# Moving one product of each attention block from VectorE to GpSimd, in place

## The chip, the cores and the metric

The kernel runs on one core of a Trainium2 chip. The metric is the device time of one execution in microseconds (us); lower is better. The engines are named as the profile names them: PE is the matrix engine TensorE (PEld its weight loads), DVE is VectorE, ACT is ScalarE, POOL is GpSimd, and SP only issues DMAs.

## The reference

Four graph layers follow one another on x of 16 graphs x 1024 nodes x 128 features, with one adjacency matrix of 1024 x 1024 for all of them (about eight edges a row). Layers L0, L2 and L3 are attention layers, L1 is a graph attention with one head. An attention layer, cut to what matters here:

```
Q, K, V = h @ Wq, h @ Wk, h @ Wv              # 8 heads of 16
scores  = einsum('bnhd,bmhd->bhnm', Q, K) / sqrt(16)
attn    = softmax(where(adj == 0, -inf, scores))
x       = layer_norm(h + einsum('bhnm,bmhd->bnhd', attn, V) @ Wo + bo)
out     = layer_norm(x + relu(x @ W1 + b1) @ W2 + b2)
```

The kernel computes it from the edges alone: for each node it fetches the keys and values of its neighbours, multiplies keys by the query, sums over the 16 features of a head, takes the exponential, and weights the values by it.

## The kernel before

**Tiles.** The nodes are sorted by degree and cut into 8 blocks of 128 (`T`); the graphs are cut into 2 groups of 8 (`GR`), so a row of one group is 8 x 128 = 1024 numbers (`ROW`). A *unit* is one layer, group and block: 64 units, of which 48 are attention. Keys and values of all nodes lie in a table in HBM, 2048 numbers a row. One *chunk* is an indirect DMA that fetches 128 rows of the table, 1 MB, one row for each partition; a partition is one edge. A block is 32 nodes x 4 edges in each of 4 quarters, and each quarter has its own number of full chunks. What is left over of the four quarters is packed into one chunk that they share (`MIX`).

**Parts.** In an attention unit the chunks are worked on in five parts: three pairs of chunks, then the shared chunk alone, then one more pair (`PIECES`, into which the shared chunk is inserted at place 3). So part 3 is half as large as the others: 1024 numbers a partition against 2048.

**The loop** runs over all parts of all units in an order written out by hand. Each part goes through:

- `gathered` (L965, GpSimd): the indirect DMAs of the part three ahead (`i - 1 + AHEAD`, `AHEAD` = 4), into one of four buffers `e`. They are issued after the weighting of part i - 1, which frees the buffer.
- `products` (L977, DVE): keys times queries, from `e` and `qr` into a buffer `pr`, of which there are four. `qr` holds the queries expanded to the edges of each quarter. For the shared chunk the second operand is `qx` instead.
- `exponentials` (L1000 on DVE, then L1004 on ACT): the sum over a head's 16 features into `sc`, then its exponential `ex`.
- `weighted` (L1028, DVE), one iteration later: values times `ex`, from `e` into the same `pr`, over the product.
- `summed` (L1044, PE), two iterations after the product: matmuls that add the edges of a node up in `acc`. Two parts of one rank are summed together, after the second.

DVE's order in a block is thus P0 R0 (W of the part before) P1 R1 W0, then the closing of the unit before it (L1081 and twice L1084), P2 R2 W1 P3 R3 W2 P4 R4 W3, with P for L977, R for L1000, W for L1028.

**`qx`** is one buffer in a pool of one (`queries_of_shared`). `shared(u)` fills it from `qr` with two to four DMAs on SP's queue (L943), in the second iteration of a block, when `qx` is free. SP works in order, and ahead of these copies stand, in layers L0 and L2, the stores of the unit that is being finished (L575, L592, L617), which wait for ACT. In layer L3 there are no such stores, and the results leave by scatters on GpSimd's queue (L699).

**Around it.** While these parts run, PE and ACT also do the rest of the unit before (its projections, norms and feed-forward part) and prepare the queries of the next one, a few steps between the parts. GpSimd also adds each unit's sums into `seen` (L1097), two operands in SBUF of 128 numbers a partition.

Of the kernel before, what the change touches and what calls it, by code (L numbers as in the profile page):

```python
# [18 lines left out]
ALU = mybir.AluOpType  # L19
# [29 lines left out]
ROW = G * D  # L49
# [17 lines left out]
MIX = J  # L67
# [51 lines left out]
def of_piece(v, piece):  # L119

    a, b = piece[0][0], piece[-1][0]
    if len(piece) == 2 and a == b:
        return v[:, a : a + 1].to_broadcast([v.shape[0], 2, v.shape[2]])
    return v[:, a : b + 1 : max(b - a, 1)]
# [21 lines left out]
def sparse_path(ctx: ExitStack, tc: tile.TileContext, a: dict, out: bass.AP, flag):  # L146


    nc = tc.nc
# [64 lines left out]
    def gather_buffer():  # L214
        return gathers.tile([P, max(4 * ROW, J * (ROW + G))], F32, tag="e", name="e")
# [646 lines left out]
    parts = []  # L862
# [7 lines left out]
    es, prs, exs, qs, qx, ofs, accums = {}, {}, {}, {}, {}, {}, {}  # L870

    def is_attention(u):
        return LAYERS[units[u][0]][1] is ATTN
# [76 lines left out]
    def gathered(i):  # L950
        if i >= len(parts):
            return
        u, pieces = parts[i]
        if u == T:
            while slow:
                while busy[0] and not held[0]:
                    advance(tails)
                advance(slow)
        l, g, t = units[u]
        width = tables[l, g].shape[1]  # L960
        many = 2 if is_attention(u) else J
        e = gather_buffer()
        es[i] = e[:, : many * width].rearrange("p (k c) -> p k c", k=many)
        for k, (j, r) in enumerate(sum(pieces, [])):
            nc.gpsimd.indirect_dma_start(  # L965
                out=es[i][:, k, :], out_offset=None, in_=tables[l, g][:, :],
                in_offset=bass.IndirectOffsetOnAxis(
                    ap=idx[:, min(l, 1), t, COLUMN[t, j, r] : COLUMN[t, j, r] + 1], axis=0
                ),
                bounds_check=N - 1, oob_is_err=False,  # L970
            )

    def products(i):
        u, (piece,) = parts[i]
        n = len(piece)
        prs[i] = [prods.tile([P, 2, ROW], F32, tag="pr", name="pr")]
        nc.vector.tensor_tensor(  # L977
            prs[i][0][:, :n, :], es[i][:, :n, :ROW],
            qx[u].rearrange("p (o c) -> p o c", o=1) if (MIX, 0) in piece
            else of_piece(qs[u], piece),  # L980
            ALU.mult,
        )

    def exs_of(i):

        u, pieces = parts[i]
        t = units[u][2]
        c, n = PLACE[(t, *pieces[0][0])], sum(map(len, pieces))
        return exs[u][:, c : c + n, :], n
# [116 lines left out]
    def advance(gens):  # L1106
        for gen in list(gens):
            got = next(gen, "end")
            if got == "end":
                gens.remove(gen)  # L1110
            elif got == "free":
                free.append(gen)
# [58 lines left out]
    with tc.manual_schedule():  # L1171
        wide = [gather_buffer() for _ in range(EDGES)]
        setup, entry, weights = graph(wide), at_once(0), load_weights("L0")
        next(setup)
        next(weights)
        next(entry)
        more = [weights, load_graph_weights()]
        rest = slots()
        first, second = loaded(0), loaded(1)
        for i, room in enumerate(setup):  # L1180
            if i == T:
                for gen in more:
                    next(gen)
            if room == "load":
                next(first)
            elif room == "spread":
                for _ in entry:
                    pass
                next(rest)
            elif room == "slots":  # L1190
                next(rest)
                for _ in first:
                    pass
                for _ in queries(0):
                    pass
                slow.append(at_leisure(1))
            elif room == "gather":
                for k in range(AHEAD - 1):
                    gathered(k)
                next(second)  # L1200
            else:
                for _ in range(room):
                    if next(entry, "end") == "end":
                        advance(slow)
                        break
        scratch.close()
        prods = ctx.enter_context(tc.tile_pool(name="prods", bufs=4))
        smalls = ctx.enter_context(tc.tile_pool(name="smalls", bufs=3))
        nc.gpsimd.memset(wide[3], 0.0)
        gathered(AHEAD - 1)  # L1210
        fronts.extend([islice(rest, WAIT + 2), second] + more)
        closing, sizes = None, ()
        begun = 0
        for i in range(len(parts) + 2):
            here = i < len(parts)
            u = parts[i][0] if here else len(units)
            if here:
                l = units[u][0]
                eager[0] = 1 if u < 2 else 0
                if i and parts[i - 1][0] != u:  # L1220
                    begun = i
                    if u < T - 1:
                        fronts.append(islice(rest, WAIT + 2))
                    if l + 1 < len(LAYERS) and LAYERS[l + 1][1] is ATTN:
                        if units[u][1:] == (0, 1):
                            more = load_weights(LAYERS[l + 1][0])
                            next(more)
                            next(more)
                        if units[u][1:] == (0, 4):
                            fronts.append(more)  # L1230
                if is_attention(u):
                    products(i)
            if i > 1:
                summed(i - 2)
                done = parts[i - 2][0]
                if parts[i - 1 : i] == [] or parts[i - 1][0] != done:
                    closing = divided(done)
                    next(closing)
            others()
            if here:  # L1240
                exponentials(i)
            if here and i == begun + 1:
                if is_attention(u):
                    shared(u)
                while loads:
                    advance(loads)
                if u + 1 < len(units):
                    fronts.append(queries(u + 1))
                loads.append(loaded(u + 2))
                if u:  # L1250
                    advance(loads)
            others()
            if 0 < i <= len(parts):
                weighted(i - 1, 0)
                if not is_attention(parts[i - 1][0]):
                    others()
                    weighted(i - 1, 2)
                gathered(i - 1 + AHEAD)
                for _ in sizes:
                    pass  # L1260
            if closing is not None and here:
                while any(gen not in free for gen in tails):
                    if opening[0] is None:
                        advance(tails)
                    else:
                        planned("ab")
                while opening[0] is not None and opening[0] < len(plan[0]):
                    planned()
                next(closing)
                sizes, closing = closing, None  # L1270
                passes = 3 if is_attention(u) else 4
                steps = STEPS if is_attention(done) else GRAPH_STEPS
                steps -= LATE[units[done][0]]
                pace[:] = 0.0, steps / (passes * sum(part[0] == u for part in parts) - 1)
                if is_attention(done) and opening[0] is None:
                    for gen in list(tails):
                        if gen in free:
                            for _ in gen:
                                pass
                            tails.remove(gen)  # L1280
                opening[0] = 0 if is_attention(done) else None
                plan[0] = PLANS.get(units[done][0], ())
            others()
            if i + 1 >= len(parts) or parts[i + 1][0] != u:

                while fronts:
                    advance(fronts)
        while opening[0] < len(plan[0]):
            planned()
        while tails:  # L1290
            advance(tails)
        for _ in closing:
            pass
        while tails:
            advance(tails)
# [435 lines left out]
```

## Time and profile before

| | |
|---|---|
| median of 3 runs | 2157.91 us (2153.96 to 2158.05) |
| profiled execution | 2143.22 us |
| its span, and mean granted PE clock | 2141.5 us, 0.97 |
| busy: PE, DVE, ACT, POOL | 91%, 86%, 71%, 49% |
| indirect gathers L965 | 576, 1569 ns mean, 8.1 us from issue to landing |
| copies into `qx`, L943 | 114 DMAs; 6.7 us to landing at 256 KB |
| all DMA | 636.10 MB, 297 GB/s over the span |

A row of a group in the profile gives line, engine, operation, output and inputs by their tile names, the shapes as partitions x elements, the count, and then busy us in total and mean ns of one; after the second bar stands the time that the engine was idle just before, and what ended most of it. A row of a timeline gives the start from the span's begin, the duration, engine, line, operation, and in brackets the idle time before it and its releaser. The first 110 us sort the graph, then come L0, L1, L2 and L3; the third layer fills most of 1000 to 1554 us. The durations shown come from this one execution.

### The profile page before, as it was taken

Reading aid. Unit: us, or ns where it says so; the run is one execution under the profiler, and the core shown is the slowest. Engines: PE = TensorE matmul, PEld = TensorE weight load, DVE = VectorE, ACT = ScalarE, POOL = GpSimd, SP = SyncE. Lnnn points to the kernel's source line nnn. Section 1 sums busy time; section 2 is a strip of 40 time slices with the busy share of each in tenths; the row PEclk is TensorE's granted clock in tenths of the full one; section 3 lists DMA queues with packets and bytes.
Section 4 is the critical chain, followed back from the end, with each engine's and each line's share of the span. In section 5 each row is a group of like instructions: output and inputs, shape, how many; then the busy total and the mean of one; then the engine's idle time right before and its main releaser. Section 6 shows DMA issues by size and latency. Waiting matters only on the chain.

```text
span 2141.5 us, 37070 instructions
## 1 busy us (share of the span) xinstructions
PE 1954.5 (91%) x13444; PEld 1237.4 (58%) x13444; DVE 1852.2 (86%) x1368; ACT 1522.8 (71%) x5043; POOL 1048.6 (49%) x699
## 2 busy tenths in 40 slices
PE   6769999999999988997999999999998999898986
PEld 5545666666655555554566565666655555555554
DVE  6977999999997666677899999999998998989993
ACT  3437878878886554555687887778886878776874
POOL 3333445555456576784354544444443545545540
PEclk8789999999999999999999999999999999999998
DMA  7978888988988799998898998989988878687860
GB/s 272 348 271 291 309 300 313 312 287 316 318 314 288 271 324 323 347 376 309 295 338 310 334 312 293 321 324 319 320 303 297 288 277 297 233 311 260 313 227 22
DMA packets 164800, 636.10 MB, mean 297 GB/s; under 512 B 34664, under 2 KB 37480, under 8 KB 116110
## 3 DMA queue, kind: packets, MB, share of 16 engines
q0 software_dynamic: 88720, 485.08, 63.5%
q1 hardware_dynamic: 75888, 148.57, 20.5%
q8 instruction: 108, 1.77, 0.3%
q14 instruction: 84, 0.69, 0.1%
HBM read 581.08 MB, written 92.34 MB: 314 GB/s over the span
## 4 chain that ended last, share of the span: by engine, by line
PE 68%; DVE 11%; ACT 8%; issue 6%; DMA 4%; POOL 2%; POOLq 0%; DVEq 0%; ACTq 0%
PE acc L1044 17%; PE yps L752 7%; PE ps L654 7%; PE ps L738 7%; PE ps L583 6%; PE ps L929 6%; PE yps L728 4%; PE yps L727 4%; DMA e<-table,idx 4%; PE yps L756 3%; DVE pr L1028 3%; PE ps L920 2%; DVE pr L977 2%; DVE sc L1000 2%; ACT qr L932 2%
## 5 line engine op out<-in xcount | busy, mean ns | idle before, releaser
L965 POOL DMA_INDIRECT e<-table,idx x576 | 903.6, 1569 | 899.0 <-DVE pr L1028 708.8
L1028 DVE TENSOR_TENSOR pr<-e,ex 128x2048 f32<-128x2048 f32 (+1 forms) x320 | 662.2, 2077 | 56.8 <-ACT ex L1016 29.6
L1044 PE MATMUL acc<-pr,marks 128*32 128x512 f32 x2656 | 516.1, 605 | 36.3 <-DVE pr L1028 18.3
L977 DVE TENSOR_TENSOR pr<-e,qr 128x2048 f32<-128x2048 f32 x192 | 441.8, 2301 | 83.2 <-PE acc L1044 30.4
L1000 DVE TENSOR_REDUCE sc<-pr 128x128 f32<-128x2048 f32 (+1 forms) x240 | 497.4, 2073 | 8.1
L631 ACT ACTIVATE z<-yps,root 128x128 f32<-128x128 f32 x888 | 312.9, 368 | 70.4 <-PE yps L756 55.6
L1044 PEld LDWEIGHTS acc<-pr,marks 128*32 128x32 f32 x2656 | 109.7, 110 | 297.6 <-issue 246.9
L752 PE MATMUL yps<-W,f 128*128 128x128 f32 x1520 | 253.6, 285 | 16.9 <-ACT f L747 16.9
L752 PEld LDWEIGHTS yps<-W,f 128*128 128x128 f32 x1520 | 203.4, 191 | 99.3 <-ACT f L747 60.2
L647 ACT ACTIVATE z<-yps,rstd 128x128 f32<-128x128 f32 x888 | 251.0, 367 | 1.6
L587 ACT COPY kv<-ps 128x512 f32<-128x512 f32 x176 | 102.8, 588 | 175.3 <-PE ps L583 160.0
L932 ACT COPY qr<-ps 128x512 f32<-128x512 f32 x384 | 202.9, 602 | 22.2 <-PE ps L929 19.9
L583 PE MATMUL ps<-Wkv,xT 128*128 128x256 f32 x768 | 204.1, 409 | 12.7 <-ACT xT L660 5.5
L747 ACT ACTIVATE f<-ps,b 128x512 f32<-128x512 f32 x190 | 130.4, 687 | 87.9 <-PE ps L738 87.8
L738 PE MATMUL ps<-x,W 128*128 128x512 f32 x384 | 187.0, 610 | 1.3 <-ACT x L662 1.3
L631 ACT ACTIVATION_READ_ACCUMULATOR z<-yps,root 128x1 f32 x888 | 184.4, 208 | 0.0
L583 PEld LDWEIGHTS ps<-Wkv,xT 128*128 128x128 f32 x768 | 145.1, 201 | 67.5 <-issue 14.0
L654 PE MATMUL ps<-ident,z 128*128 128x128 f32 x896 | 148.9, 283 | 37.1 <-ACT qr L932 27.5
L654 PEld LDWEIGHTS ps<-ident,z 128*128 128x128 f32 x896 | 106.1, 142 | 89.0 <-ACT qr L932 62.3
L929 PE MATMUL ps<-q,rep 32*128 32x512 f32 x768 | 146.7, 663 | 8.6 <-ACT q L924 7.6
L727 PE MATMUL yps<-Wo,oT 128*128 128x128 f32 x768 | 153.2, 282 | 0.2
L728 PE MATMUL yps<-centre,x 128*128 128x128 f32 x768 | 152.6, 281 | 0.5 <-ACT x L723 0.2
(174 smaller groups left out, 2526.1 us busy)
## 6 DMA issues: line engine op xcount, KB each, us to landing
table<-kv SPq DMA_DIRECT2D x88, 512.0 KB, 7.5
kept<-xT SPq DMA_DIRECT2D x96, 256.0 KB, 5.1
x<-kept SPq DMA_DIRECT2D x48, 512.0 KB, 7.9
qx<-qr SPq DMA_DIRECT2D x54, 256.0 KB, 6.7
e<-table,idx POOLq DMA_INDIRECT x576, 8.1
table<-kv SPq DMA_DIRECT2D x32, 256.0 KB, 8.1
qx<-qr SPq DMA_DIRECT2D x48, 128.0 KB, 5.0
qx<-qr SPq DMA_DIRECT2D x12, 384.0 KB, 4.6
```

The costliest lines, as they stand in the source:

```text
L583: nc.tensor.matmul(ps[:, k, :], x[:, i + k, :], w[LAYERS[l][0], "Wkv"], start=True, stop=True,)
L631: nc.scalar.activation(z[:, i, :], y[:, i, :], AF.Square, scale=D**-0.5, bias=root, accum_out=total[:, i : i + 1],)
L647: nc.scalar.activation(z[:, i, :], y[:, i, :], AF.Copy, scale=rstd[:, i : i + 1])
L654: nc.tensor.transpose(ps[:, i, :], z[:, i, :], ident)
L738: nc.tensor.matmul(ps, p["W1"][:, f * P : (f + 1) * P], x1.rearrange("p g n -> p (g n)"), start=True, stop=True,)
L752: nc.tensor.matmul(ps[:, i, :], f1[:, f, i * P : (i + 1) * P], p["W2"][:, f, :], start=(f == 0), stop=False,)
L929: nc.tensor.matmul(ps, rep_of(j), q[32 * j : 32 * j + 32], start=True, stop=True)
L965: nc.gpsimd.indirect_dma_start(out=es[i][:, k, :], out_offset=None, in_=tables[l, g][:, :], in_offset=bass.IndirectOffsetOnAxis(ap=idx[:, ...
L977: nc.vector.tensor_tensor(prs[i][0][:, :n, :], es[i][:, :n, :ROW], qx[u].rearrange("p (o c) -> p o c", o=1) if (MIX, 0) in piece else of_p ...
L1000: nc.vector.tensor_reduce(sc[:, :n, :], prs[i][0][:, :n, :].rearrange("p k (a d) -> p k a d", d=HD), mybir.AxisListType.X, ALU.add,)
L1028: nc.vector.tensor_tensor(prs[i][k0 // 2][:, :m, :].rearrange("p k (a d) -> p k a d", d=d), es[i][:, k0 : k0 + m, base : base + ROW].rearr ...
L1044: nc.tensor.matmul(outs[32 * j : 32 * j + 32], marks[:, mark, :], rhss, start=(chunk == mine[0]), stop=(chunk == mine[-1]),)
```

## The change

For a shared chunk, `products` no longer does anything: a new function `product_of_shared` multiplies on GpSimd, in place in `qx`, and enters `qx` as that part's product buffer. It is called at the end of each iteration, for the part two ahead, right after the gathers that the iteration issues. The shared chunk is part 3, so the call falls into the iteration of part 1, the same in which `shared(u)` issues the copies into `qx`. From there on the reduction reads `qx`, the weighting writes into `qx`, and the matmuls of `summed` read it; `pr` is used by the four pairs alone.

```diff
     def products(i):
         u, (piece,) = parts[i]
+        if i in prs:
+            return
         n = len(piece)
         prs[i] = [prods.tile([P, 2, ROW], F32, tag="pr", name="pr")]
         nc.vector.tensor_tensor(
             prs[i][0][:, :n, :], es[i][:, :n, :ROW],
-            qx[u].rearrange("p (o c) -> p o c", o=1) if (MIX, 0) in piece
-            else of_piece(qs[u], piece),
+            of_piece(qs[u], piece),
             ALU.mult,
         )
+
+    def product_of_shared(i):
+
+        if i >= len(parts):
+            return
+        u, pieces = parts[i]
+        if not is_attention(u) or (MIX, 0) not in pieces[0]:
+            return
+        own = qx[u].rearrange("p (o c) -> p o c", o=1)
+        prs[i] = [own]
+        nc.gpsimd.tensor_tensor(own, es[i][:, :1, :ROW], own, ALU.mult)
...
                 gathered(i - 1 + AHEAD)
+                product_of_shared(i + 2)
                 for _ in sizes:
                     pass
```

## The prediction

> **What bounds the kernel now.** I read the shares by engine first, then the chain, then one stage by windows, because the shares average over stages with different limits.
>
> ```profile
> PE 1954.5 (91%) x13444; PEld 1237.4 (58%) x13444; DVE 1852.2 (86%) x1368; ACT 1522.8 (71%) x5043; POOL 1048.6 (49%) x699
> ...
> PE 68%; DVE 11%; ACT 8%; issue 6%; DMA 4%; POOL 2%; POOLq 0%; DVEq 0%; ACTq 0%
> ```
>
> PE leads in both, but its ends are modelled: a run of 128x128 matmuls shows 0.28 us each and starts one every 0.11 us. So the windows of the third layer (columns: PE, PEld, DVE, ACT, POOL, clock, DMA share):
>
> ```profile
> 1034.00:1554.00 520.00, 498.60 (x3348) 318.37 (x3347) 486.18 (x279) 415.56 (x1327) 240.76 (x150) 1.00 0.90 317
> ```
>
> DVE is 94% busy, and its ends are not modelled. The 16 DMA engines are 90% busy. GpSimd is below half. The rows by shape give the moved instruction:
>
> ```profile
> L977 DVE TENSOR_TENSOR pr<-e,qr 128x2048 f32<-128x2048 f32 x192 | 441.8, 2301 | 83.2 <-PE acc L1044 30.4 <-DMA e<-table,idx 27.1 <-ACT qr L932 22.2
> ...
> L977 DVE TENSOR_TENSOR pr<-e,qx 128x1024 f32<-128x1024 f32 x48 | 58.4, 1218 | 0.0
> ```
>
> DVE waits for buffers (PE) and gathers (DMA) at its products: three things nearly bind at once. Now one block, first DVE's timeline, then GpSimd's. Parts are 0 to 4, the shared one is 3; P is product (L977), R reduction (L1000), W weighting (L1028).
>
> ```profile
> 1024.13 2.28 DVE L1028 TENSOR_TENSOR pr<-e,ex 128x2048 f32<-128x2048 f32 x1
> ...
> 1028.13 2.28 DVE L977 TENSOR_TENSOR pr<-e,qr 128x2048 f32<-128x2048 f32 x1
> 1030.44 2.29 DVE L1000 TENSOR_REDUCE sc<-pr 128x128 f32<-128x2048 f32 x1
> 1032.64 2.28 DVE L1028 TENSOR_TENSOR pr<-e,ex 128x2048 f32<-128x2048 f32 x1
> 1034.84 1.22 DVE L977 TENSOR_TENSOR pr<-e,qx 128x1024 f32<-128x1024 f32 x1
> 1036.09 1.22 DVE L1000 TENSOR_REDUCE sc<-pr 128x64 f32<-128x1024 f32 x1
> 1038.26 2.60 DVE L1028 TENSOR_TENSOR pr<-e,ex 128x2048 f32<-128x2048 f32 x1 [0.95 <-ACT ex L1004]
> ```
> ```profile
> 1026.69 0.98 POOL L965 DMA_INDIRECT e<-table,idx  x1 [6.12 <-DVE pr L1028]
> 1027.98 0.99 POOL L965 DMA_INDIRECT e<-table,idx  x1 [0.30 <-issue]
> 1035.19 1.73 POOL L965 DMA_INDIRECT e<-table,idx  x1 [6.23 <-DVE pr L1028]
> 1037.22 0.99 POOL L965 DMA_INDIRECT e<-table,idx  x1 [0.30 <-ACT qr L932]
> 1038.24 0.46 POOL L1097 TENSOR_TENSOR seen<-seen,both 128x128 f32<-128x128 f32 x1
> ```
>
> Zero below is the end of W0, 1026.41. Then P2 runs 1.7 to 4.0, R2 4.0 to 6.3, W1 6.2 to 8.5, P3 8.43 to 9.65. Each gather waits for the W that frees its buffer. The two chunks issued at 8.78 and 10.81 are part 0 of the next block.
>
> **What the Trainium skill says.** "SBUF — State Buffer", section "Who interferes with whom": a DVE instruction with two SBUF inputs and a GpSimd instruction that reads SBUF exclude each other, whoever starts first; a reduction contends with nobody. The trace agrees: of 48 additions into `seen` (L1097), one alone takes 0.46 us, one begun under a running L1028 ends 0.315 us after it, and an L977 due at that moment takes 2.465 us, not 2.285. The last DVE line above is another such victim (2.60). The section infers that descriptor generation escapes this; the trace disagrees: 328 of 576 gathers take 0.99 us, and those begun under a running L977 or L1028 end 0.86 us after it (1.73 at 1035.19). "GPSIMD Engine Reference", section "Performance versus the Vector engine": a two-input operation of 2048 elements takes 4497 ns; half is 2.25.
>
> **The change, part by part.** *DVE loses* 48 P3 of 1.22 us, 1.25 with the hand-over: 60 us of busy time.
>
> *GpSimd gains* 48 products of 128x1024. From L1097, 0.231 us at 16 elements and 0.461 at 128: 2.05 ns an element, so 0.461 + 896 x 2.05 ns = 2.30 us, or 2.21 after the end of a DVE instruction that it waited behind. Both ends: 2.25 (skill) to 2.45. I take 2.30.
>
> *The new waits.* The product stands behind the two gathers of part 4 (done at 2.56, so ready at 2.85) and waits for the gather of part 3 (landed, 4 us or more to spare) and for the copies into `qx` (L943, on SP). From the DMA updates the last copy lands at median 5.65 in the first layer and 3.41 in the third; in the fourth, where SP runs a block ahead, far earlier, but there GpSimd is busy with the scatter L699 until about 6.5 in 8 of 16 blocks:
>
> ```profile
> 1689.26 2.93 POOL L965 DMA_INDIRECT e<-table,idx  x1 [0.30 <-DVE o L1084]
> 1692.49 0.99 POOL L965 DMA_INDIRECT e<-table,idx  x1 [0.31 <-issue]
> ```
>
> Behind the product on GpSimd stand next block's part-0 gathers; on DVE, R3 waits for it. The copies now also wait for PE's read of the old `qx`, done some 10 us before they issue in layers one and three; in the fourth they issue when it ends, near 20, over ten us before the next product wants them: nothing.
>
> *Kind A, product ready while P2 runs (17 of the 46 blocks that I could place).* It runs 4.02 to 6.23, under R2. DVE is not touched. P3 is gone, so the first gather of the next part 0 is free: ends 9.77 instead of 10.51 (-0.74). But the second, at 10.07, now falls into W2 (9.57 to 11.85) and ends 11.85 + 0.86 = 12.71 instead of 11.80. Does that delay its landing? Today the chunks land 8.6 and 11.4 us after W1 (third layer), 2.75 apart, and 15 pairs with about 3 us between issues still land 2.5 apart: the queue sets it. I charge 0.2. Landing binds the next P0 (slack median 0.12 to 0.16 in layers three and four, 0.54 in the first), so -0.54 of the -1.25 survives; a few blocks, where P0 was late for PE, gain up to 2. The PE wait of P4 (30.4 us in all) vanishes, as part 3 takes no `pr` buffer; it lies ahead of the same landing and counts only where that is slack. Mean -0.9: **-15 us**.
>
> *Kind B, ready while R2 runs (18; the first layer's rule).* The product starts at S and holds W1 until S + 2.30 - 0.135: late by S - 4.07, mean 1.75 in layer one, 0.75 to 0.9 elsewhere. Less the 0.74, plus 0.2, less what was slack: mean +0.35, **+6 us**.
>
> *Kind C, ready after W1 has begun (10, eight in layer four).* The product ends at 8.51 + 2.21 = 10.72; R3 starts at 10.82, not 8.43; the next gather starts at 11.02 and ends 12.01 instead of 10.51. +1.5 + 0.2 each: **+17 us**.
>
> Sum +8. W2 moves up by 1.25 in kind A, and `ex` of part 2 comes from ACT about then (it held W2 for 0.95 above): +2, bounds 0 and 10. Total **+10**. The profiled execution took 2143.2 (span 2141.5 and 1.7 around it), 0.7% under the median; on it 2153, and on the median 2157.9 + 10 = **2168**.
>
> **Rivals.** *Faster: relief without blocking.* If copies and scatter come early enough that nearly all blocks are kind A, 48 x -0.9 = -43; half-way there -20: 2115 to 2150. For it: DVE is fullest, the PE wait goes, GpSimd is half idle. Against: the landings of `qx`, and 90% DMA. It decides once the mean S falls below about 4.5.
> *Slower, by issue.* If the second chunk's landing follows its issue (+0.9 in A, +2.5 in B, +3.3 in C) and not the queue, my table sums to +57: 2215. Against: the pairs 2.5 apart.
> *Nothing:* gains and losses cancel, within 0.2%, about what a measurement can tell from no change. That the move does not happen is excluded: the built order has 48 fewer DVE and 48 more GpSimd instructions.
>
> **Numbers.** Forecast (+5 to +25) 0.47; slower by issue or worse copies 0.13; nothing 0.10; faster 0.30. Hence faster 0.30, same 0.10, slower 0.60. The range leaves a tenth off either end: 2124 (-34) to 2206 (+48). As both signs hold much: the likeliest case alone is 2163 to 2183.
>
> **What would show it.** Right: the GpSimd product shows 2.2 to 4.5 us; L1028 of part 1 is stretched to 3.5 to 4.4 us in layer one; R3 (L1012 in the changed kernel, where these lines stand 12 lower) waits for GpSimd in layer four; P4's wait for PE is gone; P0's wait for gathers (27.1 us) grows past 60. Wrong: W1 stays at 2.28 throughout, or P0's wait does not grow, then it is faster; gathers landing more than 3.5 us apart mean the higher rival.

## The result, and the profile after

The changed kernel takes **2146.66 us** (median, 2139.05 to 2151.85), the kernel before, measured with it, 2160.31 (2153.96 to 2162.61): a ratio of **0.9936 [0.9914, 0.9959]**, 0.64% faster. The prediction said 2168, that is 10 us slower, with a range of 2124 to 2206, and gave "faster" three chances in ten. The two first traces stand the other way round (2143.22 us before, 2151.44 after), because the profiled execution of before was an unusually quick one; where stages are compared below, a second profile of before (`x_before`, 2157.15 us) stands for it.

The page after: busy shares, and the chain that ended last.

```profile
PE 1957.1 (91%) x13444; PEld 1236.5 (58%) x13444; DVE 1831.0 (85%) x1320; ACT 1521.6 (71%) x5043; POOL 1170.5 (54%) x747
...
PE 64%; DVE 11%; ACT 8%; issue 7%; DMA 7%; POOL 2%; SPq 0%; POOLq 0%; DVEq 0%; ACTq 0%
```

DVE has 48 instructions fewer, yet only 21 of the 60 us that they took: 1852.2 to 1831.0. The rest came back as longer instructions, as DVE's rows by shape show (busy and mean, then the idle time before them and its releasers):

```profile
L1040 DVE TENSOR_TENSOR pr<-e,ex 128x2048 f32<-128x2048 f32 x256 | 618.4, 2420 | 86.2 <-ACT ex L1016 49.9 <-ACT ex L1028 13.0 <-issue 8.2
L979 DVE TENSOR_TENSOR pr<-e,qr 128x2048 f32<-128x2048 f32 x192 | 444.4, 2315 | 55.4 <-DMA e<-table,idx 21.7 <-ACT qr L932 19.9 <-ACT f L747 4.8
...
L1012 DVE TENSOR_REDUCE sc<-qx 128x64 f32<-128x1024 f32 x48 | 58.0, 1209 | 13.6 <-POOL qx L994 13.6
```

The weighting's mean went from 2293 to 2420 ns; over 256 that is 32 us. The reduction of the shared chunk waits 13.6 us for GpSimd. At the products PE has left the list (30.4 us before) and the wait for gathers is 21.7 us (27.1 before). GpSimd's row shows the new instruction:

```profile
L994 POOL TENSOR_TENSOR qx<-e,qx 128x1024 f32<-128x1024 f32 x48 | 123.3, 2569 | 78.8 <-DMA qx<-qr 51.8 <-PE ps L929 10.8 <-PE yps L728 7.3
```

Where nothing holds it, it takes 2.36 us. The same window of the third layer as before (PE, PEld, DVE, ACT, POOL, clock, DMA share):

```profile
1034.00:1554.00 520.00, 496.69 (x3304) 315.08 (x3305) 472.85 (x263) 409.20 (x1303) 276.28 (x165) 0.99 0.89 316
```

DVE has 13 us less to do in it, and no more of the layer is done: 277.2 us for each half, 276.3 and 276.2 before.

One block of the third layer after the change, first DVE, then GpSimd:

```profile
1043.46 2.28 DVE L979 TENSOR_TENSOR pr<-e,qr 128x2048 f32<-128x2048 f32 x1
1045.78 2.29 DVE L1012 TENSOR_REDUCE sc<-pr 128x128 f32<-128x2048 f32 x1
1047.98 2.28 DVE L1040 TENSOR_TENSOR pr<-e,ex 128x2048 f32<-128x2048 f32 x1
1050.18 1.21 DVE L1012 TENSOR_REDUCE sc<-qx 128x64 f32<-128x1024 f32 x1
1053.45 2.29 DVE L1040 TENSOR_TENSOR pr<-e,ex 128x2048 f32<-128x2048 f32 x1 [2.05 <-ACT ex L1016]
```
```profile
1043.32 0.99 POOL L965 DMA_INDIRECT e<-table,idx  x1 [0.30 <-issue]
1045.48 2.50 POOL L994 TENSOR_TENSOR qx<-e,qx 128x1024 f32<-128x1024 f32 x1 [1.18 <-PE ps L929]
1050.54 1.02 POOL L965 DMA_INDIRECT e<-table,idx  x1 [2.56 <-DVE pr L1040]
```

This is kind A. The product starts just ahead of P2's end, runs under R2 and ends at 1047.98, when W1 begins; W1 keeps its 2.28. The time that P3 has left open is not used: W2 waits 2.05 us for the exponential. Now a block of the fourth layer:

```profile
1708.70 2.29 DVE L1012 TENSOR_REDUCE sc<-pr 128x128 f32<-128x2048 f32 x1
1710.90 4.50 DVE L1040 TENSOR_TENSOR pr<-e,ex 128x2048 f32<-128x2048 f32 x1
1715.33 1.21 DVE L1012 TENSOR_REDUCE sc<-qx 128x64 f32<-128x1024 f32 x1
```
```profile
1705.30 1.02 POOL L699 DMA_INDIRECT out<-outs,places  x1 [4.28 <-ACT ex L1016]
...
1709.86 0.99 POOL L965 DMA_INDIRECT e<-table,idx  x1 [0.31 <-issue]
1710.87 2.37 POOL L994 TENSOR_TENSOR qx<-e,qx 128x1024 f32<-128x1024 f32 x1
1715.67 1.02 POOL L965 DMA_INDIRECT e<-table,idx  x1 [2.43 <-DVE pr L1040]
```

The product, late behind the scatter, starts 0.03 us before W1 is due, and W1 takes 4.50 us instead of 2.28; 15 of the layer's 16 blocks show a stretched W1, 24 us in all. By the lengths of DVE's and GpSimd's instructions, the fourth layer has got worse. It got *faster*. So the gain has to come from the waits between the instructions, or from the transfers behind them.

### The profile page after: what moved, and what is told of

Read it like the earlier page. It is cut to its first block, busy times and chain, and to the rows that moved or that the text cites. A ratio compares the mean times of both kernels' runs of the same rounds, so it can differ in the third digit from the quotient of the medians.

```text
span 2149.7 us, 37324 instructions
## 1 busy us (share of the span) xinstructions
PE 1957.1 (91%) x13444; PEld 1236.5 (58%) x13444; DVE 1831.0 (85%) x1320; ACT 1521.6 (71%) x5043; POOL 1170.5 (54%) x747
## 4 chain that ended last, share of the span: by engine, by line
PE 64%; DVE 11%; ACT 8%; issue 7%; DMA 7%; POOL 2%; SPq 0%; POOLq 0%; DVEq 0%; ACTq 0%
PE acc L1056 15%; PE ps L654 7%; PE ps L738 7%; PE yps L752 7%; PE ps L583 7%; PE ps L929 5%; DMA e<-table,idx 4%; PE yps L728 4%; PE yps L727 4%; PE yps L756 3%; DVE pr L1040 3%; DVE pr L979 3%; DVE sc L1012 3%; PE ps L920 2%; POOL e L965 2%
## 5 line engine op out<-in xcount | busy, mean ns | idle before, releaser
L1040 DVE TENSOR_TENSOR pr<-e,ex 128x2048 f32<-128x2048 f32 x272 | 636.6, 2350 | 86.2 <-ACT ex L1016 49.9
L979 DVE TENSOR_TENSOR pr<-e,qr 128x2048 f32<-128x2048 f32 x192 | 444.4, 2315 | 55.4 <-DMA e<-table,idx 21.7
L1056 PE MATMUL acc<-pr,marks 128*32 128x512 f32 x2200 | 427.1, 609 | 29.7 <-DVE o L1096 15.0
L1012 DVE TENSOR_REDUCE sc<-pr 128x128 f32<-128x2048 f32 x192 | 438.9, 2286 | 6.5
L1056 PEld LDWEIGHTS acc<-pr,marks 128*32 128x32 f32 x2200 | 91.8, 110 | 253.9 <-issue 206.2
L994 POOL TENSOR_TENSOR qx<-e,qx 128x1024 f32<-128x1024 f32 x48 | 123.3, 2569 | 78.8 <-DMA qx<-qr 51.8
```

What stands on the lines that cost most here:

```text
L979: nc.vector.tensor_tensor(prs[i][0][:, :n, :], es[i][:, :n, :ROW], of_piece(qs[u], piece), ALU.mult,)
L1012: nc.vector.tensor_reduce(sc[:, :n, :], prs[i][0][:, :n, :].rearrange("p k (a d) -> p k a d", d=HD), mybir.AxisListType.X, ALU.add,)
L1040: nc.vector.tensor_tensor(prs[i][k0 // 2][:, :m, :].rearrange("p k (a d) -> p k a d", d=d), es[i][:, k0 : k0 + m, base : base + ROW].rearr ...
L1056: nc.tensor.matmul(outs[32 * j : 32 * j + 32], marks[:, mark, :], rhss, start=(chunk == mine[0]), stop=(chunk == mine[-1]),)
```

## The experiments

The theory formed from the two traces: the gain is a side effect of working in place. `qx` is now read by PE, so the copies into it (L943) wait longer, and in the fourth layer they leave the stretch in which they stood beside the gathers. Its rivals: DVE's relief; the `pr` buffer that part 3 no longer takes. The prediction's own cost, the mutual exclusion, is tested beside them.

All ratios are to the kernel before, with 95% intervals; stage times are from one profile each, from the first reduction of a layer to its last (or to the next layer's first). L1 is left out: no kernel changes it, and it varies from 316 to 327 us between profiles, and the two profiles of before differ by 6 to 7 us in L0 and in L3, so differences of that size in one stage say little. `x_noqx`, `x_memset` and `x_pe` leave work out, and are there to test a cause.

| kernel | ratio | L0 | L2 | L3 |
|---|---|---|---|---|
| x_before | 1 | 579 | 554 | 560 |
| first profile of before | | 572 | 553 | 554 |
| x_after | 0.9939 [0.9924, 0.9954] | 579 | 555 | 541 |
| x_dve_inplace | 0.9893 [0.9872, 0.9913] | 576 | 554 | 536 |
| x_pool_pr | 1.0023 [1.0009, 1.0037] | 576 | 556 | 561 |
| x_half | 0.9997 [0.9979, 1.0015] | 578 | 555 | 562 |
| x_late | 0.9882 [0.9848, 0.9916] | 576 | 554 | 536 |
| x_loadlate | 0.9975 [0.9959, 0.9992] | 574 | 555 | 557 |
| x_noqx | 0.9888 [0.9843, 0.9932] | 577 | 553 | 546 |
| x_early | 0.9889 [0.9859, 0.9919] | 571 | 553 | 543 |
| x_memset | 0.9867 [0.9836, 0.9898] | 572 | 553 | 543 |
| x_pe | 0.9738 [0.9694, 0.9783] | 566 | 549 | 533 |
| x_mix | 0.9853 [0.9815, 0.9890] | 569 | 553 | 537 |

**The two kernels as they are**, for a second profile of each.

> The kernel before, unchanged, for a second profile. Its first profiled execution (2143.2 us) lies 0.8% under the median of its runs (2160.3). If that execution was an unusually quick one, this profile has a span of 2150 to 2162 us, with the excess spread over the layers; if the profile itself makes it quick, the span is near 2142 again. In the first case the fourth layer (halves 279.3 and 274.4 us in the first profile) and the first (265.4 in its second half) are longer here.

> The changed kernel, unchanged, for a second profile and a tighter ratio: 0.9936 again, within 0.990 to 0.997. If the landings of part 0's gathers are set by the queue of DMAs and not by their issue, the profile again has second chunks of the fourth layer issued near 14.6 us after the end of W0 and landed near 19.6 us; if the first profile was an accident, 21 us or more.

The ratio repeats (0.9939). The 19 us between these two fourth layers (560 and 541) are more than the whole gain of some 14; in the two first profiles it is 11 (554 and 543). No other stage of the table shows a gain.

**The change taken apart.** `x_dve_inplace` works in place, but on VectorE:

```diff
+        if (MIX, 0) in piece:
+            own = qx[u].rearrange("p (o c) -> p o c", o=1)
+            prs[i] = [own]
+            nc.vector.tensor_tensor(own, es[i][:, :1, :ROW], own, ALU.mult)
+            return
```

> The product stays on DVE, in its old place, but is made in place in qx, as in the changed kernel: part 3 takes no pr buffer, and the copies into the next qx wait for PE. GpSimd has no product. Buffer theory (the gain comes from the pr buffer that part 3 no longer takes, 30 us of waits of P4 for PE, and from the copies that leave the neighbourhood of part 0's gathers): 0.988 to 0.995, as fast as the changed kernel or faster, since no W1 is blocked. Relief theory (the gain comes from 60 us less work on DVE): 0.998 to 1.002. Copies alone: the fourth layer is 6 to 10 us shorter, the others unchanged, 0.996.

`x_pool_pr` uses GpSimd, but a buffer of `pr`, so that `qx` is free as early as before (against the changed kernel):

```diff
-        prs[i] = [own]
-        nc.gpsimd.tensor_tensor(own, es[i][:, :1, :ROW], own, ALU.mult)
+        prs[i] = [prods.tile([P, 2, ROW], F32, tag="pr", name="pr")]
+        nc.gpsimd.tensor_tensor(prs[i][0][:, :1, :], es[i][:, :1, :ROW], own, ALU.mult)
```

> The product goes to GpSimd two parts ahead, as in the changed kernel, but is written into a pr buffer of its own, not into qx: the engine is changed, the buffers are not, and qx is free as soon as GpSimd has read it. Relief theory: as the changed kernel, 0.992 to 0.996. Buffer theory: P4 waits for PE as before (10 us a layer), W1 is still blocked by GpSimd, so 1.000 to 1.012.

In place without GpSimd gains 1.07%, more than the change; GpSimd without in place loses 0.23%. On top of in place the engine costs 0.9939 - 0.9893 = 0.46%, about 10 us (6 between the two medians, 2143.69 and 2137.47). So the move to GpSimd, which the change is named for, is its loss, and the other half, "in place", is its gain.

**What of "in place" gains.** It does two things: it spares a `pr` buffer, and it delays the copies. `x_half` only spares the buffer, with one of its own for part 3 (`both` gives up a buffer to make room; what that costs by itself was not tested):

```diff
+        if (MIX, 0) in piece:
+            prs[i] = [halfs.tile([P, 1, ROW], F32, tag="hf", name="hf")]
...
+        halfs = ctx.enter_context(tc.tile_pool(name="halfs", bufs=1))
```

> The kernel before, with the shared chunk's product on DVE in a half-size buffer of its own (one of 4 KB a partition; the tile 'both' goes from three to two buffers to make room). Part 3 takes no pr buffer, as in the changed kernel, but qx is free after P3 as before, so the copies into qx stay where they were, beside part 0's gathers in the fourth layer. If the pr buffer is what counts: 0.989 to 0.992, the fourth layer 15 to 22 us shorter than the 559.9 us of the second profile of before, waits of P4 for PE gone. If it is the place of the copies: 0.998 to 1.001 and a fourth layer of 554 us or more. If each has a share: 0.993 to 0.997.

`x_late` only delays the copies, and with them the load behind them (L895), and only in the fourth layer, by 256 bytes sent ahead of them on SP's queue to a scratch tensor `nowhere`, which wait for the last exponential of the block before:

```diff
         qx[u] = queries_of_shared()
+        if units[u][0] == len(LAYERS) - 1 and u - 1 in exs:
+            last = PLACE[(units[u - 1][2], *PIECES[units[u - 1][2]][-1][-1])]
+            nc.sync.dma_start(nowhere[:, :], exs[u - 1][0:1, last, 0:64])
```

> The kernel before, with one DMA of 256 bytes on SP ahead of the copies into qx, in the fourth layer alone; it reads the exponentials of the unit before, which ACT has made only near 16.5 us after W0, so the copies leave their place beside part 0's gathers (issue near 9.7) and go some 7 us or more later. Buffers and engine as before. If the place of the copies counts: fourth layer 8 to 15 us shorter, 0.993 to 0.996. If the pr buffer alone counts: no change, 0.998 to 1.002, P4 still waits for PE.

The buffer is worth nothing (0.9997), the delay alone everything (0.9882, and 24 us off the fourth layer, where I had expected 8 to 15), and the two together, in `x_dve_inplace`, no more than the delay (0.9893). DVE's products in the fourth layer, the rows of `x_before`, `x_half` and `x_late`, each over that layer, for the first two with the row of the weighting:

```profile
L977 DVE TENSOR_TENSOR pr<-e,qr 128x2048 f32<-128x2048 f32 x63 | 145.3, 2306 | 34.5 <-DMA e<-table,idx 17.3 <-PE acc L1044 13.0 <-PE ps L654 1.8
L1028 DVE TENSOR_TENSOR pr<-e,ex 128x2048 f32<-128x2048 f32 x64 | 147.1, 2298 | 4.2 <-ACT ex L1004 3.6
```
```profile
L980 DVE TENSOR_TENSOR pr<-e,qr 128x2048 f32<-128x2048 f32 x64 | 149.3, 2333 | 26.4 <-DMA e<-table,idx 15.1 <-PE ps L654 4.3 <-ACT ex L1007 3.5
L1031 DVE TENSOR_TENSOR pr<-e,ex 128x2048 f32<-128x2048 f32 x64 | 147.1, 2299 | 11.2 <-ACT ex L1007 11.2
```
```profile
L981 DVE TENSOR_TENSOR pr<-e,qr 128x2048 f32<-128x2048 f32 x63 | 145.7, 2312 | 9.9 <-DMA e<-table,idx 5.9 <-PE acc L1048 3.9
```

With the spare buffer the 13.0 us for PE are gone, but the gathers' wait stays (15.1) and 11.2 us for ACT appear at the weighting (3.6 before): the block ends no earlier. With the copies late, the gathers' wait falls to 5.9 and PE's to 3.9 with it. The lengths of DVE's instructions in the layer add up to the same (527.8 us in `x_before`, 527.9 in `x_late`); its waits go from 41.1 to 18.8 us.

Why, the order of the transfers tells. First `x_before`, SP and GpSimd, around one block of the fourth layer, and DVE's wait that follows:

```profile
1709.26 7.38 SPq L943 DMA_DIRECT2D qx<-qr  x2
1716.69 0.59 SPq L895 DMA_DIRECT2D x<-kept  x1
```
```profile
1707.48 1.73 POOL L965 DMA_INDIRECT e<-table,idx  x1 [2.60 <-DVE pr L1028]
1709.52 0.99 POOL L965 DMA_INDIRECT e<-table,idx  x1 [0.31 <-ACT qr L932]
...
1712.30 2.87 POOL L965 DMA_INDIRECT e<-table,idx  x1
1715.48 1.00 POOL L965 DMA_INDIRECT e<-table,idx  x1 [0.30 <-issue]
```
```profile
1726.71 2.29 DVE L977 TENSOR_TENSOR pr<-e,qr 128x2048 f32<-128x2048 f32 x1 [1.34 <-DMA e<-table,idx]
```

The 7.38 span both copies, the second issued at 1716.1. The first is issued between part 0's two chunks and the second while part 1's last is being issued, both chunk pairs for the block that follows; then comes a load of 512 KB. P1 at 1726.71 waits for its gather. In `x_late` and in the changed kernel SP's lines are these:

```profile
1680.40 1.14 SPq L947 DMA_DIRECT2D qx<-qr  x2
1681.58 0.88 SPq L896 DMA_DIRECT2D x<-kept  x1
```
```profile
1699.92 1.13 SPq L943 DMA_DIRECT2D qx<-qr  x2
1701.11 0.69 SPq L895 DMA_DIRECT2D x<-kept  x1
```

Medians over 13 blocks of the fourth layer, in us after the W0 of the block before, from the DMA records (for the copies the median of all; the first of a block is issued at 12.0, 23.9 and 28.2). The period, from one end of W0 to the next, is the mean of the layer's 15:

| | x_before | x_late | x_after |
|---|---|---|---|
| copies issued | 14.0 | 24.8 | 28.9 |
| part 0's first chunk issued | 8.8 | 8.8 | 11.0 |
| part 0 landed | 20.0 | 18.9 | 19.6 |
| part 1's first chunk issued | 13.7 | 14.5 | 16.7 |
| part 1 landed | 27.9 | 24.9 | 25.8 |
| mean period of a block | 35.4 | 33.8 | 34.1 |

In the changed kernel part 0's gather starts 2.2 us later, and yet lands 0.4 us earlier; part 1's starts 3.0 later and lands 2.1 earlier. The copies no longer stand beside them.

The granted PE clock is a rival: over the fourth layer it was 0.970 in `x_before` and 0.987 in `x_late`. But the nine blocks that ran at full clock in both traces took 35.4 and 33.9 us in the mean, 1.5 us less, and all fifteen 1.6 us less. So the clock is not what shortens the blocks.

**Is it the copies or the load behind them?** `x_loadlate` puts the same 256 bytes behind the copies, so that the load alone is late; the edit is the three added lines of `x_late`, moved to the end of `shared`.

> The kernel before, with the same waiting DMA of 256 bytes on SP in the fourth layer, but behind the copies into qx and ahead of the load of x (L896 here, 512 KB): the copies stay near 9.7 to 20 us after W0, the load goes from 18.6 to 24 or later. If the copies are what delays the gathers: fourth layer 554 to 562 us, 0.998 to 1.002. If the load behind them is: fourth layer 535 to 542, 0.987 to 0.992. If both: in between, 0.993 to 0.996.

`x_noqx` issues no copies, and multiplies the shared chunk by one quarter's queries:

```diff
-            qx[u].rearrange("p (o c) -> p o c", o=1) if (MIX, 0) in piece
-            else of_piece(qs[u], piece),
+            of_piece(qs[u], [(QUARTERS[units[u][2]][0][0], 0)] if (MIX, 0) in piece else piece),
...
-                if is_attention(u):
-                    shared(u)
```

> The kernel before, without the copies into qx: the shared chunk is multiplied, on DVE, by the queries of one quarter straight from qr (for the other quarters' edges the wrong queries, so the output is not the reference's). It takes 0.5 MB of some 11.5 MB of DMA off each attention unit, wherever it stood, and leaves the engines' work as it was. If the DMAs pace the third layer: its halves go from 277 to 263 to 272 us, and the fourth layer is as with late copies or shorter, 530 to 537; 0.975 to 0.984. If PE or ACT paces it: 275 to 277, and 0.987 to 0.990 from the fourth layer alone.

The load alone gives a quarter of a per cent, 557 us in the fourth layer, against 536 with both late. Without any copies L0 and L2 are as ever and the fourth layer is 546: so the copies cost time only in the fourth layer, where they are issued 12 to 18 us after W0 and meet the gathers; in L0 and L2 they are issued near 33 us in `x_before` already. That no copies show a longer fourth layer than late copies is a difference between two profiles; the medians of the two kernels, 2136.48 and 2134.17 us, hardly differ. And `x_noqx` changes one thing more: with nothing ahead of it on SP, the load of 512 KB goes at 10.5 us instead of 18.6. There part 0 lands at 19.9 us, as in `x_before` (20.0), and part 1 at 24.8, as in `x_late` (24.9). That the early load now delays part 0 would fit this, but is not tested; how the gain of late copies divides between copies and load stays open to that extent.

**The exclusion.** `x_memset` puts three memsets of `qx`, somewhat longer together than the product (2.9 us against 2.4), in its place; the product is left out.

```diff
-        nc.gpsimd.tensor_tensor(own, es[i][:, :1, :ROW], own, ALU.mult)
+        for _ in range(3):
+            nc.gpsimd.memset(own, 0.0)
```

> The changed kernel, with the product replaced by three memsets of qx on GpSimd: the same place, the same waits, near the same length (some 2.7 us), but nothing read from SBUF; the product of the shared chunk is left out, so the output is not the reference's. If the exclusion of two SBUF readers is what stretches W1: L1040 falls from 2.42 to 2.29 us, no stretched W1 is left, GpSimd is not held behind P2, and the time falls to that of the in-place product on DVE or below, 0.983 to 0.990. If the stretch comes from something else (the wait of R3, or plain bandwidth): as the changed kernel, 0.992 to 0.996.

`x_early` moves the copies one iteration ahead, meant to make more products of kind A:

```diff
+            if here and i == begun and is_attention(u):
+                shared(u)
             if here and i == begun + 1:
-                if is_attention(u):
-                    shared(u)
```

> The changed kernel, with the copies into qx issued one iteration earlier (in part 0's, not part 1's). In layers one and three they should land before P2 ends, so that GpSimd's product runs under R2 in every block (kind A) and W1 takes 2.28 us; in the fourth layer GpSimd is held by the scatter as before, so W1 stays near 4.3. If blocking of W1 and waits of R3 are what GpSimd costs in the first layer: its second half goes from 272 or 273 us to 265 to 269, ratio 0.988 to 0.992. If these layers are bound by something else (the third layer takes 277 us in every kernel so far): the first layer does not move, 0.993 to 0.996.

The rows of DVE for the weighting and for R3, first of `x_memset`, then of `x_early`:

```profile
L1041 DVE TENSOR_TENSOR pr<-e,ex 128x2048 f32<-128x2048 f32 x256 | 584.6, 2288 | 112.3 <-ACT ex L1017 69.4 <-ACT ex L1029 24.6 <-PE acc L1057 7.2
...
L1013 DVE TENSOR_REDUCE sc<-qx 128x64 f32<-128x1024 f32 x48 | 58.3, 1215 | 14.8 <-POOL qx L995 14.8
```
```profile
L1040 DVE TENSOR_TENSOR pr<-e,ex 128x2048 f32<-128x2048 f32 x256 | 616.8, 2414 | 80.1 <-ACT ex L1016 53.0 <-ACT ex L1028 13.0 <-ACT z L647 4.5
...
L1012 DVE TENSOR_REDUCE sc<-qx 128x64 f32<-128x1024 f32 x48 | 58.0, 1209 | 4.5 <-POOL qx L994 4.5
```

Memsets read nothing: no weighting is stretched (2288 ns), though R3 waits for GpSimd no less than in the changed kernel (14.8 and 13.6). The ratio falls to 0.9867 from 0.9939: 0.7% goes when GpSimd reads nothing from SBUF, and the wait at R3 is not what goes. Where in the kernel it goes the profile does not show: it is of the slowest of this kernel's six runs, and its fourth layer, in which most of the stretch had been, takes 543 us, where the changed kernel takes 543 and 541.

`x_early` did not do what I expected. In place of all 16, 9 blocks of L0 and 11 of L2 are of kind A (6 and 10 in the first trace of the change), and 25 weightings are still stretched (2414 ns in the mean). What goes is 9 of the 13.6 us that R3 waited, and with it 6 us of the second half of L0 (273.0 to 266.9) and half a per cent of the whole (0.9889 against 0.9939, intervals apart). So the wait at R3 seems to have a price of its own beside the stretched weighting; how the 0.46% of GpSimd divides between the two, these runs do not show.

And `x_memset`, with 60 us less work on DVE and no exclusion, is no faster than `x_late` with all of it (0.9867 and 0.9882, intervals overlapping; the copies are late in both): DVE's relief bought nothing that these ratios can tell. It comes out as waiting for ACT at the weighting, 69.4 us where `x_before` has 28.8.

**What then paces the third layer?** `x_pe` is `x_late` without the matmuls that add the residuals (`centre`) to `yps`, in all layers.

```diff
-            nc.tensor.matmul(ps[:, i, :], oT[:, i, :], p["Wo"], start=True, stop=False)
-            nc.tensor.matmul(ps[:, i, :], xt[:, i, :], centre, start=False, stop=True)
+            nc.tensor.matmul(ps[:, i, :], oT[:, i, :], p["Wo"], start=True, stop=True)
...
-            nc.tensor.matmul(ps[:, i, :], x1[:, i, :], centre, start=False, stop=True)
```

> The kernel with the late copies (x_late), without the 32 matmuls of 128x128 in each attention unit that add the residual through 'centre' (L728 and L756): the residual is left out, so the output is not the reference's. It takes 32 x 0.11 = 3.5 us of PE off each unit and nothing off DVE or the DMAs. If PE's own work paces the third layer (277 us in each of its halves in every kernel so far, with or without the product on DVE): halves of 255 to 268 us, 0.95 to 0.97. If it is paced by the gathers' DMAs: 275 to 278 us, as x_late, 0.986 to 0.990.

It gains 30 us on `x_late`, spread over the stages (9 in L0, 8 in the tail after the last reduction), but only 5 in the third layer, where I had expected at least 9 a half if PE paces it. This does not clear PE: the granted clock over that layer fell from 0.988 in `x_late` to 0.963, which over 550 us can have taken back up to 14 us of the gain (an estimate, 0.025 x 550). The layer takes 549 to 556 us in every kernel here: with the product on DVE, on GpSimd or left out, with the copies as before, 3 us earlier (`x_early`) or left out. None of these, taken away alone, shortens it by more than 6 us. Two that bind together would not show in such runs, and ACT was not tested; what paces the layer stays open.

**A version from what was found.** `x_mix` takes GpSimd with early copies in L0 and L2, where they shorten the wait at R3, and VectorE in place, with the late copies that follow from it, in the fourth layer (against the changed kernel; `products` gets the branch of `x_dve_inplace`):

```diff
         own = qx[u].rearrange("p (o c) -> p o c", o=1)
+        if units[u][0] + 1 == len(LAYERS):
+            return
...
+            if here and i == begun and is_attention(u) and l + 1 < len(LAYERS):
+                shared(u)
             if here and i == begun + 1:
-                if is_attention(u):
+                if l + 1 == len(LAYERS):
                     shared(u)
```

> A candidate: in the first and third layer as the changed kernel with the copies one iteration earlier (GpSimd makes the product); in the fourth the product stays on DVE, in place in qx, so the copies are late there and no W1 is stretched. If the two gains add: fourth layer 536 us instead of 543, 0.984 to 0.987. If the fourth layer with late copies is bound by something other than DVE: 0.987 to 0.990, no better than either alone.

2127.22 us, 0.9853 [0.9815, 0.9890], with 537 us in the fourth layer, as expected if the two gains add: the fastest of the kernels that leave no work out, and faster than the change, though its interval overlaps those of `x_late` and `x_early`. `x_late`, four lines against the kernel before, has nearly all of it.

## Why the prediction was wrong

**The step that failed** is a sentence in "The new waits": the copies in the fourth layer "issue when it ends, near 20, over ten us before the next product wants them: nothing". I asked who waits for the copies and found nobody. I did not ask what they stand beside. They issue at 28.9 in the median, not near 20, where before it was 14.0, and this takes half a megabyte a block, and the load behind it, out of the stretch in which the next block's first four chunks come in, in a layer whose products wait for them. The delay is worth -25 us alone (`x_late`: 1.18% of 2159; of this the load by itself makes 5, by `x_loadlate`), where I wrote zero. A figure of my own could have warned me: I had noted that P0's slack in the fourth layer was 0.12 to 0.16 us, and so that any transfer moved there counts.

**What the engine move costs** was near, in sum, and partly by luck, as the kinds below show. On GpSimd instead of DVE, with the buffers alike, it is +10 us in place (`x_after` against `x_dve_inplace`) and +5 (2 to 8) with the old buffers; the forecast for the whole change was +10. -23 for in place and +10 for GpSimd make the -13 that was measured.

**By kind.** By the start of the product in the first trace of the change, 17 blocks are of kind A, 25 of kind B and 6 of kind C; the prediction had 17, 18 and 10 (which is 45, not the 46 that it names). *A*: "-0.9 each" does not show. The chunks issue as worked out (in the third layer the medians of their ends are about 10.4 and 13.3 over all blocks, and 9.8 and 12.9 in kind A, against 9.77 and 12.71), W2 moves up, but the third layer, with 10 of its 16 blocks of this kind, stays at 277 us a half. Why is open, as what paces that layer is. *B*: right in direction; L0's second half goes from 265.4 and 266.9 to 272.3 and 273.0 us, +5 to +8, where I had +6 for all blocks of this kind. *C*: did not come as put: eight were to fall into the fourth layer, and none did. I took 0.30 us between the gather and the product; it is 0.02, so behind a scatter the product of the fourth layer starts at 6.20, just ahead of W1 at 6.23, and becomes a kind B of the worst sort, with W1 at 4.50. Over the layer this costs DVE 1.5 us a block in the mean, near C's 1.7; but against `x_dve_inplace` the layer loses only 5 to 7 us, where I had +17. One reason is that a chunk issued late lands less late: part 0's first is issued 2.2 us later than in `x_before` and lands 0.6 later (16.0 and 16.6).

**Right in size**: the product's duration (2.30 forecast, 2.36 measured) and its end 2.2 us after a DVE instruction that held it (2.21 forecast, though the figures given for it, 0.315 + 896 x 2.05 ns, make 2.15); the exclusion in both directions, as the Trainium skill has it ("SBUF — State Buffer", section "Who interferes with whom"): 4.50 us is 2.28 and 2.22 more, and without a read on GpSimd's side it is 2.28. The estimate from "GPSIMD Engine Reference", section "Performance versus the Vector engine", 2.25 us, was 5% low. P4's wait for PE went, as said, and was worth nothing by itself: `x_half` has no such wait, waits for the gathers and ACT in its place, and is no faster.

**The signs named in advance.** "P0's wait does not grow, then it is faster" is the one that spoke: 27.1 us (23.2 in `x_before`) became 21.7, not 60. R3's wait for GpSimd in the fourth layer, a sign for the forecast, is 0.0 there; the 13.6 us are all in L0 and L2. And the steps that rest on "the queue sets the landing" were half right: chunks landed within some 3 us of each other (16.6 and 19.6 in the fourth layer), so not by their issue, the higher rival's case (whose +57 I cannot work out again: the charges beside it, times the blocks, make 93); but what stood in the queue beside them I held to be fixed.

**The rival "faster"** had the right sign for a wrong reason: it wanted nearly all blocks to be of kind A, and with the change 25 of 48 have a stretched W1. That 2146.66 lies within its 2115 to 2150 is luck.

## What to carry to other kernels

A buffer's new reader can move the transfer that refills it: price that transfer twice, by who waits for it and by what it will stand beside, above all where the next gathers have no slack. Before an edit of two parts is judged, do each alone: here the part in the name cost half a per cent, and the side effect gained one. In this kernel a copy that is wanted only much later was better issued after the gathers that are wanted next, though it could go at once.

## What the runs showed of the hardware that I had not expected

- Between a gather's issue and a two-input instruction on GpSimd lie 0.02 us (1709.86 + 0.99 to 1710.87), not the 0.30 that lie between two gathers; this 0.28 decided between kinds C and B. The prediction's own lines had shown it: a gather at 1037.22 that takes 0.99, and L1097 at 1038.24.
- Which plain copies run beside indirect gathers matters though the DMA engines are not full: in the fourth layer of `x_before` the DMA share is 0.80 (window 1594 to 2046), and moving 0.5 MB a block (and the load behind it) by 11 us shortens a block from 35.4 to 33.8 us. In `x_late` the share is 0.86.
- A second chunk whose issue ended 3 us later (14.9 against 11.8) landed 0.4 us earlier: from the end of its issue to its landing it took 8.2 us in the fourth layer of `x_before`, and 4.7 in `x_after` (6.9 in `x_late`, where the chunk is issued as early as in `x_before`).
